# Attention and a routed expert layer on one core: the last stage's first loads, its first output projection and its gathers change places

## The chip, the core and the metric

The kernel runs on one core of a Trainium2 chip. The metric is the device time of one launch in microseconds (us). TensorE (PE in the profile) multiplies matrices into eight PSUM banks, VectorE (DVE) and ScalarE (ACT) read those banks, GpSimd (POOL) masks tiles and issues the gathers, and the queue of SyncE (SP) issues nearly all other transfers. Each engine takes its instructions in the order in which the program holds them. It stops at an instruction whose semaphores have not been reached, and all that stands behind that instruction stops with it.

## The reference, cut to what matters

```python
x = L0_attn_x                                  # (4, 1024, 512), float32
xn = _layernorm(x, axis=-1)
x = x + _L0_attn_ref(xn, Wq, bq, ...) + _L0_ffn_ref(xn, gate_w, w1, w2)

def _L0_attn_ref(x, ...):                      # 16 heads of 32
    scores = einsum('bhqd,bhkd->bhqk', q, k) / sqrt(D)
    scores = where(causal, -inf, scores) + alibi_bias
    out = einsum('bhqk,bhkd->bhqd', softmax(scores), v)
    return out.reshape(B, S, E) @ Wo.T + bo

def _L0_ffn_ref(x, gate_w, w1, w2):            # 8 experts, each token takes 2
    topw, sel = top_k(softmax(x @ gate_w.T), 2)
    topw = topw / sum(topw)
    g, u = split(x @ w1[e].T)                  # 512 -> 2 * 352
    expert_out = (silu(g) * u) @ w2[e].T       # 352 -> 512
    return sum over the two chosen experts of topw * expert_out
```

The output row of a token is thus the sum of four things: the input row, the output projection of its attention row, and two expert rows, each times its share.

## The kernel before

There are 4,096 tokens, that is 32 tiles of 128 rows, 8 tiles for each of 4 batches. Attention is worked in 16 units (b, c): one batch and a chunk c of four heads. Each unit has 12 steps g, and in each step the program writes down, in this order:

- `values(*behind)`: the product of probabilities and values of the step before (o, L1043), which DVE adds to the running sum `oT` (L1058, or a copy at L1055 for the first step of a half);
- `scores(b, c, g)`: the scores s (L969, L980, L988), which ACT turns into probabilities `pr` (L1000) and POOL masks on the diagonal (L1008);
- `largest` of the next unit: products m (L855), which DVE reduces to row minima (L879, here called the minima);
- `fill(...)`: pieces of other work, taken from the list `fills`.

The list `fills` holds the expert layer (71 blocks of 128 rows; pieces `gate`, `up` and `second_layer` for each) and then the last stage. `second_layer(k)` calls `down(k - 1)`: the product ye (L738), the addition of a bias row on DVE (yr, L747), the store of the block into the DRAM tensor `ys_d` (L748) and the loads of the next block's w2. `gate(k)` first turns the activations of block k - 1 (pact L724, evicted to actT at L727 and L730). Every piece carries a weight in us, and `fill` takes pieces while the sum of weights stays below `rate` times the number of steps so far, so that the last piece falls into the last step. `rate` is the sum of all weights over 204 steps.

The last stage makes the output rows. `final_pieces(b)` has three functions. `load(i)` issues on SP the load of the input rows `xr` (L781) and, for batches 0 to 2, of the attention rows `ot` that were parked in DRAM (L786); it also issues on POOL two gathers from `ys_d` (g, L790). `piece(i)` adds the two gathered rows, times their share, to `xr` on DVE (L812), and then projects: y (8 matmul records, L802), the addition of y to `xr` on DVE (L805) and the store (L806). For batch 3 there is no `ot`; its tiles only take the gathered rows (a join), and `rest(i)` projects them when their attention is done. The tiles are worked in the order tile 0, 1, 2, join of tile 24, tile 3, 4, 5, join of tile 25, and so on. `prime` loads the first three, and each later piece loads the tile three places ahead. There are eight buffers `g` and four each of `xr` and `ot`.

The expert pieces live in a pool `ex`, the last stage in a pool `fin` that is opened by `begin_final` in the memory that `ex` leaves. A first access to a `fin` tile waits for what last used that memory. The eight PSUM banks of attention, experts and last stage come from one pool; a product waits until the bank that it is given has been read by DVE or ACT.

The experts' last products and the last stage's first stand in unit 14, that is batch 3 and chunk 2. PE's order there is: pact and ye of block 70 in step 0, then o, s, m, the first y in step 1, and one or two y in each step after that.

Of the kernel before, what the change touches and what calls it, by code (L numbers as in the profile page):

```python
# [9 lines left out]
F32 = mybir.dt.float32  # L10
# [6 lines left out]
P = 128  # L17
# [11 lines left out]
def kernel(  # L29
# [18 lines left out]
    T, E = x.shape  # L48
# [4 lines left out]
    NC = E // P  # L53
    NT = T // P
    ST = S // P
    QB = 512
    NQ = S // QB
    QT = QB // P
# [54 lines left out]
    with ExitStack() as actx:  # L113
        wp = actx.enter_context(tc.tile_pool(name="wp", bufs=1))
        qkv = actx.enter_context(tc.tile_pool(name="qkv", bufs=1))
# [8 lines left out]
        def bank(shape, dtype, name):  # L124
            return banks["ring"].tile(shape, dtype, tag="s", name=name)
# [108 lines left out]
        xnT, qs, ks, vs, oTs, mTs = {}, {}, {}, {}, {}, {}  # L234
# [539 lines left out]
        def final_pieces(b):  # L774

            held = {}

            def load(i):
                t = b * ST + i
                xr = phase["fin"].tile([P, E], F32, tag="xr" if b < B - 1 else "held", name=f"xr{t}", bufs=4 if b < B - 1 else ST)  # L780
                nc.sync.dma_start(xr, x[t * P : (t + 1) * P, :])  # L781
                o = None
                if b < B - 1:
                    o = phase["fin"].tile([P, NC, P], F32, tag="ot", name=f"ot{t}", bufs=4)
                    cols = slice((i % QT) * P, (i % QT + 1) * P)
                    nc.sync.dma_start(o, o_d[b * NQ + i // QT][:, :, cols])  # L786
                gs = []
                for j in range(TOP):
                    g = phase["fin"].tile([P, E], F32, tag="g", name=f"g{t}_{j}", bufs=8)
                    nc.gpsimd.indirect_dma_start(  # L790
                        out=g[:, :],
                        out_offset=None,
                        in_=ys_d[:, :],
                        in_offset=bass.IndirectOffsetOnAxis(ap=slot[:, j, t : t + 1], axis=0),
                    )
                    gs.append(g)
                held[i] = xr, o, gs

            def project(t, xr, lhsTs):
                y = bank([P, E], F32, name=f"y{t}")  # L800
                for c in range(NC):
                    nc.tensor.matmul(  # L802
                        y, lhsT=lhsTs[c], rhs=wo_sb[:, c, :], start=(c == 0), stop=(c == NC - 1)
                    )
                nc.vector.tensor_tensor(xr, y, xr, ALU.add)  # L805
                nc.sync.dma_start(out[t * P : (t + 1) * P, :], xr)  # L806

            def piece(i):
                t = b * ST + i
                xr, o, gs = held[i]  # L810
                for j in range(TOP):
                    nc.vector.scalar_tensor_tensor(  # L812
                        xr, gs[j], share[:, t, j : j + 1], xr, ALU.mult, ALU.add
                    )
                if o is not None:
                    project(t, xr, [o[:, c, :] for c in range(NC)])

            def rest(i):
                cols = slice((i % QT) * P, (i % QT + 1) * P)
                project(  # L820
                    b * ST + i, held[i][0], [oTs[b, c, i // QT][:, cols] for c in range(NC)]
                )

            return load, piece, rest

# [248 lines left out]
        def final_all():  # L1076
            ops = [final_pieces(b) for b in range(B)]

            order = [(ops[b], i) for b in range(B - 1) for i in range(ST)]
            for i in range(ST):  # L1080
                order.insert(i * B + B - 1, (ops[B - 1], i))
            ahead = 3

            def prime():
                for ops_, i in order[:ahead]:
                    ops_[0](i)

            res = [prime]
            for k, (ops_, i) in enumerate(order):

                def one(k=k, ops_=ops_, i=i):
                    if k + ahead < len(order):
                        nxt, ni = order[k + ahead]
                        nxt[0](ni)
                    ops_[1](i)

                res.append(one)
            return res, ops[B - 1][2]

        phase = {}  # L1100

# [5 lines left out]
        def begin_final():  # L1107
            phase["ctx"].close()
            phase["fin"] = actx.enter_context(tc.tile_pool(name="fin", bufs=2))

        finals, rest = final_all()


        PROJ, JOIN = 3.6, 1.5
        fills = [(0.0, begin_experts)] + expert_pieces() + [(0.0, begin_final), (3.0, finals[0])]
        fills += [(JOIN if k % B == B - 1 else PROJ, f) for k, f in enumerate(finals[1:])]
        fills += [(PROJ, lambda i=i: rest(i)) for i in range(QT)]

        def unit_todo(n):
# [176 lines left out]
```

## Time and profile before

| | |
|---|---|
| time, median of 3 runs | 1665.13 us (1661.26 to 1668.31) |
| profiled execution, its own time | 1657.27 us |
| span of that execution in the trace | 1655.6 us |
| mean granted TensorE clock | 0.994 |
| PE busy | 1625.4 us, 98% of the span |
| DVE, ACT, POOL busy | 977.2, 894.5, 332.7 us |
| last stage, first y to end | 1479.9 to 1655.6 us |

The profiled execution is 7.9 us below the median of the runs. Sums are made against the profiled execution, and a difference is then put on the median. A timeline row shows start, duration, engine, line, operation, and in square brackets the idle time of the engine before it with what ended it. In the chain of waits a row shows start, duration, and the work or the transfer that the end of the program waited for at that time. "issue" is time in which the engine waited for nothing that the profile shows.

### The profile page before, as it was taken

The page shows a single profiled execution, that of the slowest core. Times are in us where ns is not written, and L with a number is a line of the kernel's source. Part 1 is how long each engine was busy: PE and PEld are TensorE (multiplying, and loading weights), DVE is VectorE, ACT ScalarE, POOL GpSimd, SP SyncE. Part 2 cuts the span into 40 slices and gives each one's busy share as a digit, 9 for nine tenths or more (in the row PEclk, how much of TensorE's full clock was granted, in tenths as well). Part 3 has the DMA queues.
Part 4 walks back from the last instruction along what each step waited for, and adds up shares of the span by engine and source line. Part 5 has one row for each costly group of instructions (what it writes and reads, how often), then busy time and mean ns, then how long its engine had stood idle before and what let it go on. Part 6 is the DMA issues. An engine that isn't in the chain of part 4 may idle for free.

```text
span 1655.6 us, 29261 instructions
## 1 busy us (share of the span) xinstructions
PE 1625.4 (98%) x9476; PEld 781.9 (47%) x9476; DVE 977.2 (59%) x2976; ACT 894.5 (54%) x2074; POOL 332.7 (20%) x763
## 2 busy tenths in 40 slices
PE   7979999999999999999999999999999999989999
PEld 4535544454444444544444445445444445433433
DVE  6756665555555555555555565555655555548762
ACT  4444565555646565655656565655555575645421
POOL 5600102112120101021111101020111112034661
PEclk9999999999999999999999999999999999989999
DMA  9836754546533433556542443565443434448891
GB/s 308 334 96 223 234 191 161 178 152 223 171 120 122 126 122 124 175 177 207 168 136 94 133 137 114 174 238 183 138 139 114 133 98 158 134 130 263 252 300 59
DMA packets 146489, 278.97 MB, mean 169 GB/s; under 512 B 16448, under 2 KB 45120, under 8 KB 144800
## 3 DMA queue, kind: packets, MB, share of 16 engines
q1 hardware_dynamic: 132128, 234.60, 42.7%
q0 software_dynamic: 10800, 35.40, 7.1%
q10 hardware_dynamic: 3408, 7.10, 1.2%
q8 instruction: 75, 1.23, 0.3%
q14 instruction: 78, 0.64, 0.1%
HBM read 229.07 MB, written 47.97 MB: 167 GB/s over the span
## 4 chain that ended last, share of the span: by engine, by line
PE 96%; DVE 1%; issue 1%; DMA 1%; ACT 0%; POOL 0%; SPq 0%; ACTq 0%; DVEq 0%; POOLq 0%
PE ye L738 12%; PE pup L690 11%; PE pgate L690 10%; PE s L969 10%; PE o L1043 9%; PE m L855 9%; PE pk L584 7%; PE y L802 7%; PE pq L584 7%; PE pv L616 7%; PE s L988 2%; PE pxs L683 2%; PE pact L724 2%; PE ptr L327 1%; PE plg L339 1%
## 5 line engine op out<-in xcount | busy, mean ns | idle before, releaser
L1000 ACT ACTIVATE pr<-s,kbias 128x512 f32<-128x512 f32 (+3 forms) x768 | 383.1, 581 | 426.5 <-PE s L988 426.4
L901 ACT ACTIVATE z<-z,top 128x896 f32<-128x896 f32 (+7 forms) x512 | 391.5, 774 | 77.8 <-DVE top L891 77.8
L1008 POOL TENSOR_SCALAR_AFFINE_SELECT pr<-pr 128x128 f32<-128x128 f32 x512 | 148.9, 299 | 1111.6 <-ACT pr L1000 1104.9
L879 DVE CUSTOM_DVE_ANT_0 z<-m,rel 128x512 f32<-128x512 f32 (+3 forms) x512 | 271.6, 586 | 102.4 <-PE m L855 101.7
L738 PE MATMUL ye<-w,actT 128*128 128x512 f32 (+1 forms) x426 | 199.8, 605 | 1.4 <-issue 1.4
L690 PE MATMUL pgate<-w,xsT 128*128 128x352 f32 x568 | 183.0, 465 | 3.5 <-issue 3.1
L690 PE MATMUL pup<-w,xsT 128*128 128x352 f32 x568 | 183.1, 465 | 0.0
L969 PE MATMUL s<-q,k 32*128 32x512 f32 (+3 forms) x1536 | 178.1, 533 | 0.0
L855 PE MATMUL m<-k,q 32*128 32x512 f32 (+3 forms) x1536 | 171.3, 487 | 0.7 <-DVE oT L1058 0.3
L879 DVE CUSTOM_DVE_ANT_0 z<-m,rel,l 128x128 f32<-128x128 f32 (+3 forms) x256 | 125.8, 548 | 72.5 <-PE m L855 72.5
L1043 PE MATMUL o<-pr,v 128*32 128x512 f32 (+3 forms) x1536 | 164.4, 498 | 0.1
L690 PEld LDWEIGHTS pup<-w,xsT 128*128 128x128 f32 x568 | 105.2, 190 | 71.1 <-ACT pr L1000 12.7
L690 PEld LDWEIGHTS pgate<-w,xsT 128*128 128x128 f32 x568 | 103.0, 191 | 52.6 <-issue 4.5
L584 PE MATMUL pk<-xnT,wk 128*128 128x512 f32 x256 | 120.3, 613 | 3.0 <-issue 2.8
L738 PEld LDWEIGHTS ye<-w,actT 128*128 128x128 f32 (+1 forms) x426 | 77.0, 192 | 88.9 <-issue 73.9
L584 PE MATMUL pq<-xnT,wq 128*128 128x512 f32 x256 | 118.9, 607 | 0.0
L616 PE MATMUL pv<-wv_sb,xnT 128*128 128x512 f32 x256 | 117.5, 603 | 0.0
L969 PEld LDWEIGHTS s<-q,k 32*128 32x128 f32 x1536 | 60.0, 182 | 120.6 <-issue 87.4
L855 PEld LDWEIGHTS m<-k,q 32*128 32x128 f32 x1536 | 90.9, 185 | 39.1 <-DVE oT L1058 14.0
L1058 DVE TENSOR_TENSOR oT<-oT,o 128x512 f32<-128x512 f32 (+3 forms) x160 | 83.9, 524 | 37.5 <-PE o L1043 36.8
L707 DVE SCALAR_TENSOR_TENSOR th<-th,pgate 128x352 f32<-128x352 f32 x71 | 37.0, 521 | 116.4 <-ACT th L706 116.4
L747 DVE TENSOR_TENSOR yr<-ye,bo_sb 128x512 f32<-128x512 f32 x71 | 49.1, 692 | 89.8 <-PE ye L738 89.7
(157 smaller groups left out, 1660.2 us busy)
## 6 DMA issues: line engine op xcount, KB each, us to landing
w<-in_w1T SPq DMA_DIRECT2D x284, 352.0 KB, 4.2
w<-in_w2T SPq DMA_DIRECT2D x142, 256.0 KB, 2.8
ys_d<-yr SPq DMA_DIRECT2D x71, 256.0 KB, 2.0
w<-in_w2T SPq DMA_DIRECT2D x71, 192.0 KB, 4.0
xr<-in_x SPq DMA_DIRECT2D x32, 256.0 KB, 4.3
out<-xr SPq DMA_DIRECT2D x32, 256.0 KB, 4.8
xn_d<-xT ACTq DMA_DIRECT2D x6, 1024.0 KB, 7.6
o_d<-oT SPq DMA_DIRECT2D x24, 256.0 KB, 2.3
```

Source lines behind the costliest of these rows:

```text
L584: nc.tensor.matmul(ps, lhsT=ws[which][:, i, :], rhs=xnT[b, s][:, i, :], start=(i == 0), stop=(i == NC - 1),)
L616: nc.tensor.matmul(ps, lhsT=xnT[b, t // QT][:, i, (t % QT) * P : (t % QT + 1) * P], rhs=wv_sb[:, i, :], start=(i == 0), stop=(i == NC - 1),)
L690: nc.tensor.matmul(ps, lhsT=xsT[k][:, c, :], rhs=w1s[k, c][:, gu, :], start=(c == 0), stop=(c == NC - 1),)
L738: nc.tensor.matmul(y, lhsT=a[:m, f, :], rhs=w2s.pop((k, f))[:m, :], start=(f == 0), stop=(f == NF - 1),)
L802: nc.tensor.matmul(y, lhsT=lhsTs[c], rhs=wo_sb[:, c, :], start=(c == 0), stop=(c == NC - 1))
L855: nc.tensor.matmul(pss[h][:, col : col + n], lhsT=qs[b, c, s][r, (i % QT) * P : (i % QT + 1) * P], rhs=ks[b, c, k0 // QB][r, :n], start=Tr ...
L879: nc.vector.tensor_tensor_reduce(out=zs[h][:, z0 : z0 + n], in0=pss[h][:, col : col + n], in1=rel[:, S - L + k0 : S - L + k0 + n], scale=1 ...
L901: nc.scalar.activation(z[h][:, z0 : z0 + L], z[h][:, z0 : z0 + L], AF.Exp, bias=top[:, h : h + 1], scale=-slopes[c * HC + h], accum_out=to ...
L969: nc.tensor.matmul(ps[:, :n], lhsT=ks[b, c, j // QT][r, (j % QT) * P : (j % QT + 1) * P], rhs=qs[b, c, s][r, q0:], start=True, stop=False,)
L1000: nc.scalar.activation(pr[:, :n], pss[h][:, :n], AF.Exp, bias=kbias[:, hh, d : d + 1], scale=-slopes[hh],)
L1008: nc.gpsimd.affine_select(out=pr[:, :P], in_=pr[:, :P], compare_op=ALU.is_ge, fill=0.0, base=0, pattern=[[1, P]], channel_multiplier=-1,)
L1043: nc.tensor.matmul(o[h * D : (h + 1) * D, :n], lhsT=vs[b, j][:, col : col + D], rhs=prs[h][:, :n], start=True, stop=True, skip_group_check ...
```

## The change

Three things are moved, and two weights are set anew.

- The loads of the first three tiles (`prime`) no longer use the pool `fin`. Their input rows go into the buffer that held `wv`, their attention rows into a buffer that held normalized inputs (tag `xnT`). Both had their last use before. `prime` stands three pieces before the end of the experts' list, ahead of block 69's `second_layer`.
- The first tile's projection and its addition to `xr` stand between the experts' last `gate` (which only turns block 70's activations) and the last `second_layer`, that is ahead of block 70's ye. The gathers of the first three tiles are a piece of their own (`begin`) behind `begin_final`.
- A tile's projection now comes first, its y is added to `xr`, and the two gathered rows are added after it (`join`), then the store follows. The gathers of the tile three places ahead are issued behind that. The rows of tile 0 are joined together with those of tile 1, after tile 1's projection.
- The weight of a join falls from 1.5 to 0.6, and the first load's from 3.0 to nothing, so `rate` falls from 5.003 to 4.953.

```diff
-            def load(i):
+            def load(i, xr=None, o=None):
                 t = b * ST + i
-                xr = phase["fin"].tile([P, E], F32, tag="xr" if b < B - 1 else "held", ...)
+                if xr is None:
+                    xr = phase["fin"].tile([P, E], F32, tag="xr" if b < B - 1 else "held", ...)
                 nc.sync.dma_start(xr, x[t * P : (t + 1) * P, :])
-                o = None
                 if b < B - 1:
-                    o = phase["fin"].tile([P, NC, P], F32, tag="ot", name=f"ot{t}", bufs=4)
+                    if o is None:
+                        o = phase["fin"].tile([P, NC, P], F32, tag="ot", name=f"ot{t}", bufs=4)
                     cols = slice((i % QT) * P, (i % QT + 1) * P)
                     nc.sync.dma_start(o, o_d[b * NQ + i // QT][:, :, cols])
-                gs = []
+                held[i] = xr, o
+
+            def gather(i):
+                t = b * ST + i
                 for j in range(TOP):
                     g = phase["fin"].tile([P, E], F32, tag="g", name=f"g{t}_{j}", bufs=8)
                     nc.gpsimd.indirect_dma_start(
...
-                    gs.append(g)
-                held[i] = xr, o, gs
+                    held[i] += (g,)
...
                 nc.vector.tensor_tensor(xr, y, xr, ALU.add)
+
+            def store(t, xr):
                 nc.sync.dma_start(out[t * P : (t + 1) * P, :], xr)

             def piece(i):
+                xr, o = held[i][:2]
+                if o is not None:
+                    project(b * ST + i, xr, [o[:, c, :] for c in range(NC)])
+
+            def join(i):
                 t = b * ST + i
-                xr, o, gs = held[i]
+                xr, o, *gs = held[i]
                 for j in range(TOP):
                     nc.vector.scalar_tensor_tensor(
                         xr, gs[j], share[:, t, j : j + 1], xr, ALU.mult, ALU.add
                     )
                 if o is not None:
-                    project(t, xr, [o[:, c, :] for c in range(NC)])
+                    store(t, xr)
...
-            return load, piece, rest
+            return load, gather, piece, join, rest
...
             def prime():
-                for ops_, i in order[:ahead]:
-                    ops_[0](i)
-
-            res = [prime]
-            for k, (ops_, i) in enumerate(order):
-
-                def one(k=k, ops_=ops_, i=i):
+                o = qkv.tile([P, NC, QB], F32, tag="xnT", name="ot_first", bufs=2)
+                xr = wp.tile([P, NC, E], F32, tag="wv", name="xr_first")
+                for n, (op, i) in enumerate(order[:ahead]):
+                    op[0](i, xr[:, n, :], o[:, :, n * P : (n + 1) * P])
+
+            def begin():
+                for op, i in order[:ahead]:
+                    op[1](i)
+
+            res = [prime, lambda: order[0][0][2](order[0][1]), begin]
+            for k, (op, i) in enumerate(order):
+
+                def one(k=k, op=op, i=i):
                     if k + ahead < len(order):
                         nxt, ni = order[k + ahead]
                         nxt[0](ni)
-                    ops_[1](i)
+                    if k > 0:
+                        op[2](i)
+
+                    for m in ([], [0, 1], [k])[min(k, 2)]:
+                        order[m][0][3](order[m][1])
+                    if k + ahead < len(order):
+                        nxt[1](ni)
...
-        PROJ, JOIN = 3.6, 1.5
-        fills = [(0.0, begin_experts)] + expert_pieces() + [(0.0, begin_final), (3.0, finals[0])]
-        fills += [(JOIN if k % B == B - 1 else PROJ, f) for k, f in enumerate(finals[1:])]
+        PROJ, JOIN = 3.6, 0.6
+        fills = [(0.0, begin_experts)] + expert_pieces()
+
+        fills.insert(len(fills) - 3, (0.0, finals[0]))
+        fills.insert(len(fills) - 1, (PROJ, finals[1]))
+        fills += [(0.0, begin_final), (0.0, finals[2]), (0.0, finals[3])]
+        fills += [(JOIN if k % B == B - 2 else PROJ, f) for k, f in enumerate(finals[4:])]
         fills += [(PROJ, lambda i=i: rest(i)) for i in range(QT)]
```

More of the change, by code (lines that the diff above doesn't have):

```diff
@@ L776, in final_pieces @@
             held = {}
-            def load(i):
+            def load(i, xr=None, o=None):
                 t = b * ST + i
-                xr = phase["fin"].tile([P, E], F32, tag="xr" if b < B - 1 else "held", name=f"xr{t}", bufs=4 if b < B - 1 else ST)
+                if xr is None:
+                    xr = phase["fin"].tile(
+                        [P, E],
+                        F32,
+                        tag="xr" if b < B - 1 else "held",
+                        name=f"xr{t}",
+                        bufs=4 if b < B - 1 else ST,
+                    )
                 nc.sync.dma_start(xr, x[t * P : (t + 1) * P, :])
-                o = None
                 if b < B - 1:
-                    o = phase["fin"].tile([P, NC, P], F32, tag="ot", name=f"ot{t}", bufs=4)
+                    if o is None:
+                        o = phase["fin"].tile([P, NC, P], F32, tag="ot", name=f"ot{t}", bufs=4)
                     cols = slice((i % QT) * P, (i % QT + 1) * P)
                     nc.sync.dma_start(o, o_d[b * NQ + i // QT][:, :, cols])
-                gs = []
+                held[i] = xr, o
+            def gather(i):
+                t = b * ST + i
                 for j in range(TOP):
@@ L815, in piece @@
                 if o is not None:
-                    project(t, xr, [o[:, c, :] for c in range(NC)])
+                    store(t, xr)
             def rest(i):
+                t = b * ST + i
                 cols = slice((i % QT) * P, (i % QT + 1) * P)
-                project(
-                    b * ST + i, held[i][0], [oTs[b, c, i // QT][:, cols] for c in range(NC)]
-                )
-            return load, piece, rest
+                project(t, held[i][0], [oTs[b, c, i // QT][:, cols] for c in range(NC)])
+                store(t, held[i][0])
+            return load, gather, piece, join, rest
         M_GROUPS = []
@@ L1094, in one @@
                         nxt[0](ni)
-                    ops_[1](i)
+                    if k > 0:
[4 more added lines that the diff above has]
+                        nxt[1](ni)
                 res.append(one)
-            return res, ops[B - 1][2]
+            return res, ops[B - 1][4]
         phase = {}
```

## The prediction

> **What bounds the kernel now.** I read the page first. PE is busy for 1625.4 of 1655.6 us, so only time in which PE stands still or runs slowly can be won, and every new stop of PE is lost. The list of waits, limited to PE from 1400 us to the end, then says where PE stops late in the kernel:
>
> ```profile
> PE y L802 <- DMA ot<-o_d: 3.9, 1, 3.9
> PE ye L738 <- issue: 1.4, 1, 1.4
> ```
>
> Columns: engine and line, what it waited for, us in total, times, longest. Both stand at the seam between experts and last stage. The chain of waits, in order of time, shows the seam:
>
> ```profile
> 1459.13 2.79 PE ye L738 x6
> ...
> 1466.85 1.42 issue
> 1468.27 4.36 PE ye L738 x6
> ...
> 1473.38 2.56 DMA ys_d<-yr
> ...
> 1476.47 3.29 DMA ot<-o_d
> 1479.75 0.14 issue
> 1479.89 6.22 PE y L802 x8
> ...
> 1489.77 3.63 PE y L802 x8
> ```
>
> The six records of ye took 2.79 us at 1459.13 but 4.36 us behind the wait. The eight of y took 6.22 us behind their wait and 3.63 us ten us later. The view by windows says why:
>
> ```profile
> 1468.00:1470.00 2.00, 1.73 (x2) 0.84 (x3) 0.77 (x2) 1.68 (x5) 0.00 (x0) 0.50 0.00 0
> 1480.00:1482.00 2.00, 2.00 (x3) 0.97 (x4) 0.00 (x0) 0.00 (x0) 1.39 (x3) 0.50 0.71 216
> 1512.00:1560.00 48.00, 48.00 (x265) 19.31 (x257) 40.99 (x111) 30.38 (x68) 23.80 (x34) 1.00 0.77 238
> ```
>
> The third number from the end is the granted clock, 0.50 after each of the two waits. The last row is the stage behind the seam: PE without a gap, and DVE (41 of 48 us) next to it. The timelines of POOL, DVE and PE give the prices of a join:
>
> ```profile
> 1477.96 0.94 POOL L790 DMA_INDIRECT g<-ys_d,slot  x1 [0.83 <-DVE l L879]
> 1479.21 0.95 POOL L790 DMA_INDIRECT g<-ys_d,slot  x1 [0.30 <-issue]
> 1486.58 0.75 DVE L812 SCALAR_TENSOR_TENSOR xr<-g,share,xr 128x512 f32<-128x512 f32 x1 [1.65 <-DMA g<-ys_d,slot]
> 1501.21 1.12 PE L855 MATMUL m<-k,q 32*128 32x512 f32 x2 [0.34 <-DVE oT L1058]
> ```
>
> Gathers are issued 1.25 us apart, the second landed 7.3 us after its issue, and in the last row PE waits for DVE's addition to oT, which stood behind two additions of gathered rows.
>
> **What is removed.** Block 70's ye waited because actT stood behind four minima on DVE. In the built order, gate and up of block 70 share step 0 with block 69's pact, and between block 70's pact and its ye now lie o, s, m, the first y, o and s: 1.42 us of wait and 4.36 - 2.79 = 1.57 us of slow clock go. The first y waited for its attention rows, whose load waited (second chain row) until the store of block 70 had landed, since it overwrites that pool. In the built order the six loads wait only for earlier loads, and are issued behind block 69's w2, several steps ahead of use: 3.93 us of wait and 6.22 - 3.63 = 2.59 us of slow clock go. Together 9.5 us.
>
> **What moves at no cost, and its cover.** Six loads of some 0.55 us issue each (3.3 us) now stand on SP ahead of block 69's store and block 70's w2. Those cannot go before block 69's ye has ended anyway. From there yr 0.69, store 0.34, three w2 issues 1.51 and a landing of 4.0 (page) make 6.6 us; block 70's ye comes after pt, pact, o, s, m, y, o, s, about 9.2 us. Cover 2.6 us; if a landing takes the 6.9 us that the slowest gather of expert rows took, 0.3 us are lost. The gathers go behind the masks of steps 2 and 3 on POOL instead of ahead of them, which delays no mask. The stores on SP come 1.5 us later, and the loads behind them are three tiles early.
>
> **What is added.** A new wait, on DVE. Behind tile 1's addition of y stand the joins of tiles 0 and 1, and they need four gathers, which need block 70's store. Let T be the end of block 70's ye. Before, ye ended at 1472.6 and the store had landed at 1475.9: T+3.3. POOL started the first gather 0.83 us after its last mask: I take T+4.1 (T+3.4 if the wait alone counts). The fourth is issued 3.75 us later, T+7.85. Landing: 3.7 us (least), 4.8 (the gather at 1485.46, when the loads beside it were done), 5.7 (median) and 7.3 (beside seven loads). Now three loads run beside it, so I take 4.8: it lands at L = T+12.65, with bounds T+10.85 and T+15.15.
>
> Behind the joins DVE holds the addition of o to oT (step 3), which frees a bank. In the built order the o of step 4 waits for just this bank. PE from T: pi 0.2, second y 3.6, o 0.4, s 1.3, m 0.9, a wait of 0.3 for probabilities, third y 3.6: it arrives at T+10.3, and goes on at L+1.1 = T+13.75. That is the first stop, 3.5 us. Next PE needs DVE again: the last m of step 5 takes the bank of step 4's o, which DVE frees only after oT 0.3, four minima 2.45, y's addition 0.6, two joins 1.45, the division of oT 0.7, two more joins (tile 24) 1.45 and the copy 0.7: L+8.45 in all with the last of the four additions (0.75). Without waits PE would be there at T+13.2 (o 1.0, s 1.3, three m 0.6). Both stops together cost 12.65 + 8.45 - 13.2 = 7.9 us (bounds 6.1 and 10.4).
>
> Behind the stop the fourth y runs at a slow clock: 2.6 us by the y behind the 3.93 us wait, 1.6 by the ye behind the 1.42 us wait. I take 2.6, the row with the nearer length and the same matrix. Added: 10.5 us, bounds 7.7 and 13.0.
>
> The Trainium skill ("TensorE: Matmul & The Clock Gate", Part 1) says the gate falls to half after about 3.4 us of idleness and opens after 3.4 us of work, which would make the loss at most 1.7 us and the net 0.1 instead of 1.0; the 1.42 us wait that was followed by 0.50 says that less idleness can be enough. The skill ("DMA: Bandwidth & Descriptors", Anatomy of one DMA) prices a transfer issued by GpSimd at about 2.0 us plus its bytes over 436 GB/s, 2.6 us for these 256 KB, an estimate that would bring the net to -1.2; no gather here landed under 3.3 us.
>
> **Order of the joins later on.** An addition of y now waits for y before the two joins instead of after them, and oT's addition stands behind all. Nothing is lost if the minima end no earlier than y (at 1517.6 and 1525.0 DVE took y without a wait). At five of these additions from 1498 to 1560 DVE did wait for y, 5.1 us in all (1.01, 0.95, 0.62, 0.22, 2.33): that is the upper bound. No gain: the bank that y frees sooner is followed by one that waits for oT. I take 0, since DVE is loaded for 41 of 48 us there. From the first step of unit 15 there are no minima, and PE has a y between o and the next need.
>
> **Weights.** The rate falls by 1%, so the experts end one to two steps later and pieces move against the steps everywhere. PE's total work stays. From 300 to 1460 us PE waited twice, 0.2 us each: nothing to win; one such wait in each of 14 units would be 2.8 us. I take 0.
>
> **Sum.** 1657.3 - 9.5 + 10.5 = 1658.3 us for a profiled execution; on the median 1665.1 + 1.0 = 1666.1 us. Own range by the bounds: -1.8 to +3.5 from the seam, 5.1 and 2.8 at most behind it.
>
> **Rivals.** (1) Slower, the joins' new place: if after the seam the minima end well before y in each step of unit 14, PE's last m waits for y, its addition, the joins and oT in series. It decides from the point where DVE's wait for y reaches the two joins (1.5 us); the price is up to the 5.1 us above: 1671.2 us. Against it is DVE's load; for it the five waits. (2) Faster, the gathers are quick: nothing but three loads shares the queues, they start at T+3.4 and land in 3.7 us: 6.1 us of stops, and if the clock stays full net -3.4, 1661.7 us. For it are the expert rows' gathers (median 3.6 us). Even then four issues on POOL stand before L, so the whole 9.5 us cannot be kept. (3) The loads do not come early, because the left buffers are still held: then the first y keeps its 6.5 us, 1672.6 us. The built order shows no such wait.
>
> **How the numbers follow.** The forecast has 0.58, rival 1 0.22, rival 2 0.17, rival 3 0.03. The runs before scattered by 3.9 us below and 3.2 above their median. 0.5% is 8.3 us, about what a measurement of this kernel can tell from no change. Slower by that much needs rival 1 with the late gather and the weights' price (1.0 + 5.1 + 2.5 + 2.8), or scatter on top of rival 1 or 3: 0.14. Faster by that much needs nearly all of the removed 9.5 us, which the four issues exclude, so only scatter on rival 2: 0.06. Range: rival 2 less its scatter, 1658, to rival 1 with the late gather and half the weights' price, 1675.
>
> **What would show it.** Right: ye of block 70 takes 2.8 us and the first y 3.6 to 3.7 us without a wait; PE's list of waits names DVE's oT (addition, then copy) with some 3.5 and 4.4 us; the first join waits for a gather, some 9 us after block 70's ye; the clock is 0.50 once, at the fourth y. Wrong: PE runs through step 5, or shows many waits for oT in unit 14, or the first y still waits for its load.

## The result and the profile after

The changed kernel takes 1674.74 us (median of 4 runs, 1673.63 to 1675.96); the kernel before, measured beside it, 1664.27 us (median of 4, the three runs above and one more, 1661.26 to 1668.31). The ratio is 1.0062 with a 95% interval of 1.0044 to 1.0081: some 10.4 us slower, where 1.0 us was forecast.

The timeline of PE at the seam (start, us, engine, line, operation, idle time before it and what ended it) shows that the waits that were to go have gone:

```profile
1480.73 3.70 PE L812 MATMUL y<-wo_sb,ot_first 128*128 128x512 f32 x8
...
1485.48 2.85 PE L738 MATMUL ye<-w,actT 128*128 128x512 f32 x6
...
1495.49 3.70 PE L812 MATMUL y<-wo_sb,ot_first 128*128 128x512 f32 x8
```

The first y and block 70's ye run without a wait and at full clock (before: 6.22 and 4.36 us behind waits of 3.93 and 1.42 us). The list of PE's waits, from 1400 us to the end, names what came instead:

```profile
PE m L872 <- DVE oT L1072: 10.0, 1, 10.0
PE o L1060 <- issue: 3.4, 2, 2.8
```

The chain of waits shows what DVE was doing meanwhile (start, us, what):

```profile
1488.36 0.70 DVE yr L747
1489.08 2.00 DMA ys_d<-yr
...
1497.64 0.50 DVE xr_first L829
...
1506.45 0.44 DVE oT L1078
1507.05 0.74 DVE xr L829
1507.83 0.75 DVE xr L829
1508.59 6.37 another core or an unknown queue
1514.98 0.70 DVE oT L1072
1515.73 2.07 PE m L872 x10
1517.80 5.26 PE y L812 x8
```

With T = 1488.3 us as the end of block 70's ye, the first join starts at T+9.3, PE goes on with o at T+13.6 (1501.97), and DVE has done its last addition of gathered rows at T+20.2. All that was forecast to within 0.2 us or so. Then comes a row that was not: DVE's copy of oT, which needs the o that PE's records have at 1501.97, starts 6.4 us late. The windows view (us, busy time of PE, PEld, DVE, ACT and POOL, then the granted clock, the DMA share and GB/s) has the stop between full and slow clock:

```profile
1500.00:1504.00 4.00, 2.03 (x19) 0.94 (x21) 3.80 (x10) 0.00 (x0) 3.09 (x4) 1.00 0.91 218
...
1508.00:1512.00 4.00, 0.00 (x0) 0.00 (x0) 0.58 (x1) 0.00 (x0) 3.09 (x4) 0.50 1.04 368
...
1516.00:1520.00 4.00, 4.00 (x13) 2.08 (x14) 2.97 (x16) 2.59 (x5) 0.00 (x0) 0.50 0.01 2
```

This trace can't be subtracted from that of before as it stands. The profiled execution of before (1657.27 us) was 7.0 us under its kernel's median, and that of after (1675.96 us) 1.2 us over. The two traces differ by 18.6 us, the medians by 10.4. On the three chips of the experiments below, the kernel before took 1657 us (medians 1656.9 to 1657.4), so each experiment is compared with the runs of before on its own chip.

### The profile page after: what moved, and what is told of

Same layout as the page of the kernel before. It is cut to its first block, busy times and chain, and to the rows that moved or that the text cites. A ratio compares the mean times of both kernels' runs of the same rounds, so it can differ in the third digit from the quotient of the medians.

```text
span 1674.2 us, 29253 instructions
## 1 busy us (share of the span) xinstructions
PE 1630.0 (97%) x9476; PEld 784.4 (47%) x9476; DVE 978.4 (58%) x2976; ACT 893.7 (53%) x2074; POOL 333.4 (20%) x763
## 4 chain that ended last, share of the span: by engine, by line
PE 91%; DMA 3%; DVE 2%; issue 2%; ACT 1%; POOL 0%; another core or an unknown queue 0%; SPq 0%; ACTq 0%; DVEq 0%; POOLq 0%
PE ye L738 11%; PE pup L690 10%; PE pgate L690 10%; PE s L986 9%; PE o L1060 9%; PE m L872 8%; PE pk L584 7%; PE pq L584 6%; PE y L812 6%; PE pv L616 6%; PE pxs L683 2%; PE s L1005 2%; PE pact L724 2%; DMA xr_d<-xg 1%; DMA xg<-in_x 1%
## 5 line engine op out<-in xcount | busy, mean ns | idle before, releaser
L872 PE MATMUL m<-k,q 32*128 32x512 f32 (+3 forms) x1536 | 176.6, 489 | 11.3 <-DVE oT L1072 10.0
```

The costliest lines, as they stand in the source:

```text
L872: nc.tensor.matmul(pss[h][:, col : col + n], lhsT=qs[b, c, s][r, (i % QT) * P : (i % QT + 1) * P], rhs=ks[b, c, k0 // QB][r, :n], start=Tr ...
```

## The experiments

**The weights alone.** The kernel before with two numbers changed:

```diff
-        PROJ, JOIN = 3.6, 1.5
-        ... [(0.0, begin_final), (3.0, finals[0])]
+        PROJ, JOIN = 3.6, 0.6
+        ... [(0.0, begin_final), (0.0, finals[0])]
```

> The kernel before with the two weights of the change alone (join 0.6, first load 0.0, so the rate is 4.953). The prediction priced this at 0 with 2.8 us as the most. The trace of after, laid against that of before, had lost some 5 us by the start of unit 14, ahead of the seam. If the weights cost that, this kernel takes about 1669 us, and PE shows new short waits in units 6 and 10. If the 5 us are scatter between executions (the profiled execution of before was 7 us under its median), it takes 1664 us, within 2 us of the kernel before.

Measured: 1663.45 us against 1657.33, ratio 1.0037 (1.0023 to 1.0051), 6.1 us slower. That is most of what the whole change costs. The largest losses come in single steps: 3 and 5 of unit 0, 8 of unit 10, 5 of unit 13, 1.1 to 1.7 us each. Other steps lose and gain up to 1.5 us, which cancels but for some 1.3 us. (A step is measured here and below from its o to the next o. A piece that the program writes down in step g lies behind the o of step g - 1 and is counted there.) PE's timeline of before in step 8 of unit 10 (eight records, two for each of four heads), and then of this kernel in step 5 of unit 0 and again in step 8 of unit 10:

```profile
1172.98 1.10 PE L855 MATMUL m<-k,q 32*128 32x512 f32 x8
```

```profile
237.47 2.63 PE L690 MATMUL pup<-w,xsT 128*128 128x352 f32 x8 [1.11 <-ACT pr L1000]
...
1168.23 2.20 PE L855 MATMUL m<-k,q 32*128 32x512 f32 x8
```

The same eight products m took twice as long, and no idle time stands before them. In before the products of the four heads start within 0.02 us of each other (1172.98 to 1173.00): each uses 32 rows of PE, and they run side by side. Here they start at 1168.23, 1168.24, 1168.72 and 1169.31, since the third and fourth wait for a bank that DVE has still to read (its reads of two banks end at 1168.66 and 1169.26). While only one or two quarters of PE work, the record says that PE is busy. The Trainium skill ("TensorEngine Tiling (Array Packing)", Key Properties) says that such tiles can load and multiply in parallel; the trace agrees, 1.10 against 2.20 us, and shows what is lost when their banks come one by one. The windows view of both kernels over this stretch:

```profile
1173.00:1175.00 2.00, 2.00 (x15) 0.93 (x12) 0.96 (x3) 1.76 (x4) 0.69 (x3) 1.00 0.97 314
```

```profile
1168.00:1170.00 2.00, 2.00 (x20) 1.00 (x12) 1.83 (x5) 1.62 (x5) 0.58 (x2) 1.00 0.02 8
```

PE (second number) is busy for 2.00 of 2.00 us in both, at full clock. Over units 0 to 13 the groups of m took 12.5 us more than their shortest in before and 15.3 us here. With two waits of 1.1 us for probabilities (the pup row; the other is in unit 13) that is 5.0 of the 6.1 us.

**The joins later.** The changed kernel, with the joins of the first tiles put off and all later ones a piece behind their projection (the gathers that wait for their buffers move with them):

```diff
+                    joins = ([], [], [0], [], [1, 2], [3, 4])[k] if k < 6 else [k - 1]
+                    for m in joins:
+                        order[m][0][3](order[m][1])
                     if k > 0:
                         op[2](i)
...
-                    for m in ([], [0, 1], [k])[min(k, 2)]:
-                        order[m][0][3](order[m][1])
```

> The changed kernel with the joins put later: tile 0 is joined at the third projection, tiles 1 and 2 at the fourth, tile 24 and tile 3 behind it, and every later tile one piece after its own projection, ahead of that piece's y. No join then stands in DVE's order before its gathers have landed. If the joins' place is what cost the 7.9 us of stops and 2.6 us of slow clock, PE shows no stop for oT in steps 4 and 5. If the unforeseen 6.4 us (DVE's copy of oT, which waits for a product that PE had run long before) come with the burst of gathers that four joins in a row release, they go too: 1657 us or less. If that wait comes from something else that the change did, it stays: about 1664 us.

Measured: 1674.68 us, ratio 1.0111 (1.0095 to 1.0126), 17 us slower than before and 8 us slower than the changed kernel on the same chip. PE's list of waits says why:

```profile
PE y L812 <- DMA ot<-o_d: 9.8, 5, 4.3
...
PE m L872 <- DVE xr_first L815: 1.2, 1, 1.2
...
PE m L872 <- DVE oT L1072: 0.5, 1, 0.5
```

The first stop in unit 14 is gone, and steps 3 and 4 are 5.5 us shorter than those of the changed kernel run beside it. Short stops are left in step 4 (1.2 and 0.5 us), and the y behind them takes 6.14 us, so that step is still some 6 us longer than in before. Besides, a tile's buffer `xr` is now held one piece longer, and with four of them SP's next loads stand behind stores that come later: five projections wait for their rows. The expected total was missed because I had counted neither the buffers nor the short stops.

**No second burst of gathers.** The changed kernel leaves out the eight gathers that follow the first eight; those joins add tile 24's rows again.

```diff
-                        nxt[1](ni)
+                        nxt[1](ni) if k + ahead not in (4, 5, 6, 7) else nxt[5](ni, order[3][0][6][order[3][1]][2:])
```

> The changed kernel without the eight gathers that follow the first eight; the joins of the four tiles that they belong to add the rows of tile 24 again, so DVE works as much as before. Theory that the queues' load makes the 6.4 us: DVE's copy of oT comes within 1 us of its turn, ACT's exponentials do not stand for 19 us, and the time is some 6 us under that of the changed kernel, 1668 us. Rival, that the wait lies in the order of PE and DVE: the copy still waits some 6 us and the time stays at 1674 us. Under both, PE's stops of 3.5 us (first) and some 4.4 us (second) are still there, since the first four gathers are not touched.

Measured: 1667.49 us, ratio 1.0061 (1.0047 to 1.0074), and no 6.4 us wait; the stops are there (1.9 and 3.4 us). Taken alone this would speak for the full queues. The next run takes that away.

**The changed kernel again**, twice, unaltered.

> The changed kernel once more, unaltered, for a second trace. If the 6.4 us wait of DVE's copy belongs to the change, the copy waits again 5 to 8 us beyond its turn, while the queues are full, and the time is 1673 to 1676 us. If it was an accident of one execution, the copy comes at once and the profiled time is some 6 us lower, about 1668 us.

> The changed kernel a third time, for its trace. In the first trace DVE's copy of oT waited 6.4 us while the queues were full, in the second not at all. If that wait is an event of single executions, it is absent or in another place; if it depends on the chip, it may be there again with a time 6 us higher against the kernel before (16 us instead of 9.5).

Measured: 1666.83 us (5 runs), ratio 1.0059 (1.0045 to 1.0073), 9.5 us slower than before; and one run of 1670.44 us on another chip, too few to compare. Neither trace has the 6.4 us wait. PE's timeline in the first of the two:

```profile
1500.16 1.52 PE L1060 MATMUL o<-pr,v 128*32 128x512 f32 x8 [2.31 <-DVE oT L1075]
1501.61 2.09 PE L986 MATMUL s<-q,k 32*128 32x512 f32 x8
1503.47 0.65 PE L1005 MATMUL s<-mT,ones_b 3*128 3x512 bf16 x4
1503.90 0.67 PE L872 MATMUL m<-k,q 32*128 32x256 f32 x6
1507.43 2.07 PE L872 MATMUL m<-k,q 32*128 32x256 f32 x10 [2.86 <-DVE oT L1072]
1509.43 6.10 PE L812 MATMUL y<-wo_sb,ot 128*128 128x512 f32 x8
```

These are the two stops without anything on top: 2.31 and 2.86 us (2.8 and 3.5 in the other trace). The windows view has the clock at 0.58 from 1500 to 1504 us and at 0.50 from 1508 to 1512 us. Beside full-speed rows of the same work in before (o 1.07, s 1.14 and 0.40, m 1.04, y 3.70 us), the rest of these rows lasts 5.7 us longer. DVE's timeline shows the order that makes the stops:

```profile
1496.19 1.54 DVE L829 SCALAR_TENSOR_TENSOR xr_first<-g,share,xr_first 128x512 f32<-128x512 f32 x2 [4.83 <-DMA g<-ys_d,slot]
1498.37 1.54 DVE L829 SCALAR_TENSOR_TENSOR xr_first<-g,share,xr_first 128x512 f32<-128x512 f32 x2 [0.63 <-DMA g<-ys_d,slot]
1499.82 0.28 DVE L1075 TENSOR_TENSOR oT<-oT,o 128x128 f32<-128x128 f32 x1
```

DVE stands 4.83 us at the first join, until its gather lands, and the addition to oT that PE needs is two joins further on.

**The change with the old weights.** In the changed kernel:

```diff
-        PROJ, JOIN = 3.6, 0.6
+        PROJ, JOIN = 3.6, 1.5
-        fills += [(0.0, begin_final), (0.0, finals[2]), (0.0, finals[3])]
+        fills += [(0.0, begin_final), (3.0, finals[2]), (0.0, finals[3])]
```

> The changed kernel with the weights of before (join 1.5, 3.0 for the piece that issues the first gathers, so the rate is 5.003 again). On one chip the weights alone made the kernel before 6.1 us slower and the whole change 9.5 us. If the two parts add up, the change without its weights stands 3.4 us above the kernel before, its steps in units 0, 10 and 13 are as long as before's, and DVE still waits for the first gathers in unit 14, with PE's stops for oT behind it. If the weights matter only through the seam, it stays some 9 us above.

Measured: 1664.78 us, ratio 1.0043 (1.0029 to 1.0056), 7.4 us slower, not 3.4. Up to unit 13 the steps are those of before to 0.02 us each, so all that the change lost there came from its weights. The seam was not the same, though. With these weights block 70's ye falls into step 1 of unit 14 as the program writes it, and the gathers now stand on POOL ahead of the masks of step 2. PE's and POOL's timelines:

```profile
1487.68 1.80 PE L1060 MATMUL o<-pr,v 128*32 128x256 f32 x8 [5.98 <-POOL pr L1025]
```

```profile
1479.12 0.94 POOL L801 DMA_INDIRECT g<-ys_d,slot  x1 [5.22 <-DVE l L896]
...
1485.72 1.28 POOL L801 DMA_INDIRECT g<-ys_d,slot  x1 [0.31 <-issue]
1487.01 1.34 POOL L1025 TENSOR_SCALAR_AFFINE_SELECT pr<-pr 128x128 f32<-128x128 f32 x4
```

POOL waits for the store of block 70 (the view names DVE, but the store's transfer landed at 1477.95 us, and in the traces of the changed kernel too the first gather comes 1.2 us behind that landing), issues six gathers, and only then masks the probabilities that PE has needed since 1481.7. The wait for the gathers has moved from DVE to POOL.

**Old weights and later first joins**, the others ahead of their own projection as in the kernel before (op[5] adds the gathered rows, op[6] stores):

```diff
+                    for m in {2: [0], 4: [1, 2], 5: [3, 4], 6: [5]}.get(k, []):
+                        order[m][0][3](order[m][1])
+                    if k > 5:
+                        op[5](i)
                     if k > 0:
                         op[2](i)
+                    if k > 5:
+                        op[6](i)
```

> As the kernel with the old weights, and the first joins later: tile 0 ahead of the third projection, tiles 1 and 2 ahead of the fourth, tile 24 and tile 3 ahead of the fifth, tile 4 ahead of the sixth; from there on every tile is joined ahead of its own projection, as in the kernel before, so loads and stores keep their distance. If the gain of the change (9.5 us of waits and slow clock at ye and at the first y) is real and was given back only by joins that stand on DVE before their gathers have landed, this takes 5 to 9 us less than the kernel before. If PE is only let through to the next late transfer, it lands within 2 us of it, and a new wait for a gather or a load shows in unit 14.

Measured: 1655.15 us, ratio 0.9987 (0.9978 to 0.9996), 2.2 us faster than before. The stops behind DVE's joins are gone; POOL's remains:

```profile
PE o L1066 <- POOL pr L1031: 5.4, 2, 5.0
```

**The gathers split too.** With the old weights again; `begin` issues no gathers any more, and none stands ahead of a mask that PE soon needs:

```diff
+                    for m in {4: [0, 1], 5: [2, 3], 6: [4, 5], 7: [6]}.get(k, []):
+                        order[m][0][3](order[m][1])
...
+                    early = {0: [], 1: [0, 1], 2: [2, 3], 3: [], 4: [4, 5], 5: [6, 7], 6: [8, 9], 7: [10]}
+                    for m in early.get(k, [k + ahead]):
+                        if m < len(order):
+                            order[m][0][1](order[m][1])
```

> The kernel with late first joins, and the gathers split: those of tiles 0 and 1 stand behind the masks of step 2 on POOL, those of tile 2 and tile 24 behind the masks of step 3, and none ahead of a mask that PE soon needs; tiles 0 and 1 are joined ahead of the fourth projection, tile 2 and tile 24 ahead of the fifth, the next three one or two pieces late, all others ahead of their own projection. Old weights. If the 5.0 us in which PE waited for POOL's mask, and the slow clock behind it (4.05 and 2.43 us in steps 1 and 2 of unit 14), were the last part of what the change gave back, this takes 6 to 10 us less than the kernel before, and PE shows no wait over 1 us in unit 14. If another late transfer takes their place, the gain stays near the 2.1 us of the kernel with late first joins.

Measured: 1648.90 us (1646.57 to 1649.11), ratio 0.995 (0.9936 to 0.9963): 8.0 us faster than before. PE's list of waits from 1400 us to the end, whole, and two windows:

```profile
PE m L878 <- DVE xr L815: 0.4, 1, 0.4
PE m L878 <- DVE inv L1050: 0.2, 1, 0.2
```

```profile
1474.00:1486.00 12.00, 12.00 (x91) 5.63 (x89) 6.48 (x26) 8.02 (x24) 6.87 (x13) 1.00 0.60 182
1486.00:1498.00 12.00, 12.00 (x69) 4.91 (x68) 10.64 (x21) 3.17 (x8) 7.62 (x9) 1.00 0.83 264
```

PE is busy throughout, and the clock is 1.00 all along the seam. This version beats both kernels.

**The same with the change's weights** (join 0.6, nothing for the first loads).

> The kernel with split gathers, but with the change's own weights (join 0.6, nothing for the first loads, rate 4.953). If weights and seam add up, it stands some 5 to 6 us above the kernel with split gathers and the old weights, that is 1 to 5 us under the kernel before, and ahead of unit 14 its steps are those of the changed kernel. If the weights only mattered together with the stops at the seam, it takes as little as the one with the old weights.

Measured: 1659.80 us, ratio 1.0015 (1.0006 to 1.0024), some 2.5 us slower than before and 11 us slower than with the old weights. Ahead of unit 14 its long steps are those of the weights alone (1.15 and 1.62 us more in steps 3 and 5 of unit 0, 1.10 in step 8 of unit 10, 1.61 in step 5 of unit 13). The gain was given back and more: with these weights, other joins meet other steps. Steps 5 and 7 of unit 14 are 3.3 and 5.9 us longer than in before, with two stops of PE for an addition of y on DVE (0.91 and 1.85 us) and slow rows behind them. So the parts don't add up; the weights cost 6 us by themselves, and 11 us under an order that was written for the old ones.

**Half way, and the other way.** The kernel before with join 1.05 and first load 1.5 (rate 4.978), and with 2.4 and 6.0 (rate 5.053):

> The kernel before with weights half way (join 1.05, first load 1.5, rate 4.978). If a lower rate costs in proportion, this stands 3 us above the kernel before. If the cost comes from where single pieces happen to fall against the steps (four bank waits that split a group of four products), it is not on that line: anything from 2 us below to 6 us above, with the lost time in other steps than those of the kernel with the full change of weights (steps 3 and 5 of unit 0, 8 of unit 10, 5 of unit 13).

> The kernel before with the weights moved the other way by as much (join 2.4, first load 6.0, rate 5.053). If the rate costs in proportion, this gains as much as the changed weights lost, some 6 us. If what counts is where pieces happen to fall against the steps, it gains or loses on no such line, and the steps that grow or shrink in the trace are others than with the lower rate.

Measured: ratios 1.0029 (1.0017 to 1.0041) and 1.0011 (1.0002 to 1.0021), 4.9 and 1.6 us slower. The first alone would not exclude 3 us in proportion; the second does, as a higher rate gains nothing. The groups of m over their shortest add up to 13.0 and 12.1 us (before 12.5), in other steps each time: 1.8 us in the last step of units 1 and 6 with the one, in the last of unit 10 with the other. These sums explain neither time. By step lengths less the time of their pieces, an estimate, both kernels lost some 4.5 us ahead of the last step of unit 13, whichever way the rate moved, and the second got as much back from there to the end of unit 14. That fits a cost that hangs on which piece falls into which step; beyond the groups of m and one slow pup (last section) it was not taken apart.

## Why the prediction was right or wrong

| step of the prediction | forecast, us | measured, us, and where |
|---|---|---|
| ye's wait and slow clock | -3.0 | -3.15 (last step of unit 13) |
| first y's wait and slow clock | -6.5 | -6.67 (step 0 of unit 14) |
| two stops of PE behind the joins | +7.9 | +5.2 (2.31 and 2.86) |
| slow clock behind the stops | +2.6 | +5.7 (after both, not one) |
| order of additions later on | 0, at most 5.1 | 2.8 in four steps, not taken apart |
| weights | 0, at most 2.8 | +6.1 (kernel before with the weights alone) |

The step rows come from the second trace of the changed kernel: a step's length less the time of the pieces filled into it, minus the same for before. They leave out step 1 of unit 14, which became 1.0 us shorter. Stops and slow clock together are 10.9 us against 10.5 forecast, so the seam comes out near zero, as predicted. That is partly luck: the stops were sized too long, because PE came 0.6 us later and went on 0.6 us sooner than the sum had it (T+10.9 to T+13.2, with T = 1487.0 in this trace), and the slow clock too short: it was counted for one y, but the clock was at 0.50 for 10.24 us in all (3.41 and 6.83 us here, 10.24 us on end in the third trace). The mechanism was right: the gain at ye and y is real, and the wait for block 70's gathers takes its place, first on DVE. The kernel with split gathers shows both halves, since it keeps the gain when nothing that PE needs stands behind a gather.

The step that failed is the weights: "From 300 to 1460 us PE waited twice, 0.2 us each: nothing to win; one such wait in each of 14 units would be 2.8 us. I take 0." The list of waits holds only times at which all of PE stood still. Groups of m that ran one quarter at a time were counted as busy: 12.5 us of them were in the trace of before already, and a look at the m rows (1.04 us in most steps, 2.50 in some) would have shown that there was something to lose. Worked out like the step rows, the traces with the new weights lose 6.6 to 7.8 us ahead of the last step of unit 13 (seven traces, the changed kernel's three among them), and those with the old weights and the moved work 0.0 us (three kernels). The cost has no use of its own: the experiments with other rates lie on no line.

That put the result at the upper end of the range, and on the far side of 0.5%, to which the text gave 0.14; the interval (0.44% to 0.81%) reaches over that bound. That it still lies inside the range is luck: the upper end was made of rival 1's 5.1 us, a late gather and half the weights' 2.8 us, and what was lost was mostly the weights' 6.1 us. Rival 1 named another place for the loss, the later additions; at most 2.8 us of it is there. Rival 2 had the better size for the stops (6.1 us; 5.2 and 6.3 in the two later traces), but it needed a clock that stays full, and the clock fell in all three traces. Rival 3 is excluded by the first y.

What stays open is the 6.4 us wait of DVE's copy in the first trace of the changed kernel. In that stretch the DMA share was 1.03 to 1.06 from 1506 to 1514 us, and ACT stood as well and went on at the same moment. But in the second trace the share was 0.99 to 1.08 from 1504 to 1512 us without such a wait, so full queues alone don't make it. The trace narrows it a little: the copy and ACT's exponentials wait for PE's semaphore, which shows no update from 1500.93 to 1513.55 us (in the second trace it is updated at 1501.67 us, with the end of that o). So by this record PE's word came late, and not DVE or ACT; why is not known. The other runs of that set were within 2.4 us of the profiled one; whether they had the wait can't be told, as they left no trace here.

## What to carry to other kernels

A removed wait is worth something only if nothing that the bounding engine needs stands, in any engine's order, behind the transfer that is late next: here the gathers took the wait over on DVE, then on POOL, and the 8 us came only when joins and gathers were both put behind the work that PE needed. Where products run side by side on parts of TensorE, read the length of each group against its shortest and not only the list of waits, since a group during which the engine counts as busy can still take twice its shortest time. And a weight that moves every piece of a filled schedule is a change to the whole kernel: measure it by itself.

## What the runs showed of the hardware

The length of a stop does not decide whether the clock falls. It fell after a stop of 2.31 us (second trace of the changed kernel), but stood at 1.00 after one of 2.78 us (first trace, 1500 to 1504 us) and after the 1.11 us wait for probabilities. In the kernel with half-way weights it fell 1.4 us after a stop of 0.48 us, the only one near, and a pup of 2.63 us took 4.33 us. Its timeline and windows:

```profile
371.81 1.31 PE L855 MATMUL m<-k,q 32*128 32x512 f32 x4 [0.48 <-DVE inv L1027]
373.05 4.33 PE L690 MATMUL pup<-w,xsT 128*128 128x352 f32 x8
```

```profile
374.00:376.00 2.00, 2.00 (x4) 1.01 (x3) 0.55 (x3) 1.38 (x4) 0.43 (x1) 0.50 0.94 342
```

The Trainium skill ("TensorE: Matmul & The Clock Gate", Part 1) speaks of a window of about 3.4 us that runs free of the program, which fits that like stops end differently. The clock's records here agree with such a window: the slow stretches at the seam last 3.41 and 6.83 us in before and in the second trace of the changed kernel, 10.24 in its third and 13.65 in its first, whole multiples of 3.41. The page names an idle window of that length as the condition, and elsewhere in that part short idles between groups of products, with no length for these; here the clock fell after stops that were shorter than the window, one of them 0.48 us.
